# Attention over time and over bands: scores turned to [key, query], exponentials without a maximum, masks as zeros, the division on the output

## The chip, the core and the metric

The kernel runs on one core of one Trainium2 chip. Times are device microseconds of one execution. Three runs of the kernel before took 6690.1, 6692.72 and 6694.46 us; the median, 6692.72, is the time before. Engine names are those of the profile: PE does matmuls (PEld is its loading of weights, a row of its own), ACT the activations, DVE the vector work, POOL is GpSimd, SP issues most of the DMAs.

## What is computed

Input x is [2, 256, 128, 128] float32: batch, time, band, channel. Three residual steps follow each other: causal attention over the 256 time steps of each band, attention over the 128 bands of each time step with a mask of 16 bands to either side, and a feed-forward of width 512.

```python
xt = _ln(x, ln_t_w, ln_t_b).transpose(0, 2, 1, 3)
x = x + _mha(xt, t_wi, t_bi, t_wo, t_bo, 4, causal_mask).transpose(0, 2, 1, 3)
xf = _ln(x, ln_f_w, ln_f_b)
x = x + _mha(xf, f_wi, f_bi, f_wo, f_bo, 4, band_mask)      # |i - j| <= 16
xn = _ln(x, ln_n_w, ln_n_b)
h = gelu(xn @ w1.T + b1)
x = x + (h @ w2.T + b2)
```

In `_mha` queries, keys and values have 4 heads of 32 channels; the weights are softmax(q k^T / sqrt(32) + mask). The weights of the layers are normal with a deviation of 0.02, the biases are 0 and the norms' weights 1. Everything is float32.

## The kernel before, in words

Token tiles are [128 tokens, 128 channels]; four of them (NT = 4) make a unit. In the attention over time a unit is two sequences of 256 steps, in the attention over bands four sequences of 128 bands. Each stage has 128 units. The stages follow each other through an array x1 in HBM.

The function attention (line 134) does a unit. norm_transposed normalises the tiles (statistics and xh on DVE, the power for rstd on POOL), transposes them on PE into the PSUM tile xp, and ACT copies them out as xnT with the norm's weight and bias as scale and bias (131). PE then makes qp, kp and vp (144 to 153); ACT moves qT and kT out with their biases, DVE v. The scores sp are [query, key]: for two heads at a time, PE first writes the mask with a product of a bfloat16 identity and the mask (166) and adds the scores to it (173). DVE takes the negated maximum of each row (181, 187), ACT the exponential with that maximum as bias, 128 or 256 keys at a time, with the row's sum read from its accumulator (195), DVE the reciprocal (203), and POOL multiplies the weights with it (206 over bands, 214 over time). PE transposes every block of 128x128 weights (221), DVE and ACT move the transposed blocks out as pT (226, 228), and PE multiplies with the values (239), which gives op as [channel, query]. ACT moves it out as oT with the values' bias (245), PE makes yp (248), and DVE adds it to rd, or to x2 in the second stage (249).

The first stage loads 8 bands at once and stores a unit's result as it is done. The second works in 32 blocks of 16 time steps (GB): four units of attention, then four of feed-forward (310 to 332), in which PE makes hp, ACT the gelu and PE zp. Because exponential and gelu need different tables in ACT, order_act holds each block's gelus behind its last exponential, and the next block's exponentials behind those.

A scheduler puts the instructions of each engine in order at build time, and each engine then goes through its own list. PSUM has four buffers of one bank for the tiles of the tag ps (xp, qp, kp, vp, tp, op, yp, hp, zp) and two of two banks for sp.

Of the kernel before, what the change touches and what calls it, by code (L numbers as in the profile page):

```python
# [10 lines left out]
BF16 = mybir.dt.bfloat16  # L11
AF = mybir.ActivationFunctionType
# [5 lines left out]
P = 128  # L18
H = 4  # heads
D = 32  # channels of a head  # L20
BAND = 16
EPS = 1e-5
NEG = -1e38  # a masked score, exact enough in bfloat16: its exponential is 0
NT = 4  # token tiles of 128 that are worked on together
GA = 8  # bands loaded at once for the attention over time
GB = 16  # time steps loaded at once for the attention over bands
# [3 lines left out]
def conv_seq_kernel(  # L30
# [13 lines left out]
    """x [B, T, FB, C]; weights transposed to [in, out]; cols [C, 16], the  # L44
    per-channel vectors as columns; rows [3, C], the biases added to token-major
    results."""
    nc = tc.nc
    B, T, FB, C = x.shape
    NI = w1T.shape[1] // P
    NC_T = T // P  # L50
    scale = 1.0 / math.sqrt(D)

    const = ctx.enter_context(tc.tile_pool(name="const", bufs=1))
    xpool = ctx.enter_context(tc.tile_pool(name="xpool", bufs=3))
    work = ctx.enter_context(tc.tile_pool(name="work", bufs=3))
    small = ctx.enter_context(tc.tile_pool(name="small", bufs=6))
    ps_s = ctx.enter_context(tc.tile_pool(name="ps_s", bufs=2, space=PSUM))
    ps = ctx.enter_context(tc.tile_pool(name="ps", bufs=4, space=PSUM))
    dram = ctx.enter_context(tc.tile_pool(name="dram", bufs=1, space=DRAM))

# [1 line left out]
    cols_sb = const.tile([P, 16], F32, name="cols_sb")  # L62
    nc.sync.dma_start(cols_sb, cols)
    rows_sb = const.tile([P, 3, C], F32, name="rows_sb")
    for i in range(3):
        nc.sync.dma_start(rows_sb[:, i, :], rows[i : i + 1, :].partition_broadcast(P).squeeze(1))

    def weight(src, n, name):
        t = const.tile([P, n], F32, name=name)
        nc.scalar.dma_start(t, src)  # L70
        return t

    wiT = (weight(t_wiT, 3 * C, "t_wiT_sb"), weight(f_wiT, 3 * C, "f_wiT_sb"))
    woT = (weight(t_woT, C, "t_woT_sb"), weight(f_woT, C, "f_woT_sb"))
    w1T_sb = weight(w1T, NI * P, "w1T_sb")
    w2T_sb = const.tile([P, NI, C], F32, name="w2T_sb")
    nc.scalar.dma_start(w2T_sb, w2T.rearrange("(j p) c -> p j c", p=P))

    ident = const.tile([P, P], F32, name="ident")
    make_identity(nc, ident)  # L80
    ident_b = const.tile([P, P], BF16, name="ident_b")
    nc.vector.tensor_copy(ident_b, ident)
    mhalf = const.tile([P, NT], F32, name="mhalf")
    nc.vector.memset(mhalf, -0.5)

    # masks for a bank of scores: [query, block, key]
    mask_t = const.tile([P, 3, P], BF16, name="mask_t")
    nc.gpsimd.memset(mask_t, 0.0)
    for n in (0, 2):
        nc.gpsimd.affine_select(  # L90
            out=mask_t[:, n, :], in_=mask_t[:, n, :], compare_op=ALU.is_ge, fill=NEG, base=0,
            pattern=[[-1, P]], channel_multiplier=1,
        )
    mask_f = const.tile([P, NT, P], BF16, name="mask_f")
    nc.gpsimd.memset(mask_f, 0.0)
    for s in (1, -1):
        nc.gpsimd.affine_select(
            out=mask_f, in_=mask_f, compare_op=ALU.is_ge, fill=NEG, base=BAND,
            pattern=[[0, NT], [-s, P]], channel_multiplier=s,
        )  # L100
# [3 lines left out]
    bqs = []  # L104
    for i in (2, 7):
        t = const.tile([P, 1], F32, name=f"bqs{i}")
        nc.vector.tensor_scalar_mul(t, cols_sb[:, i : i + 1], scale)
        bqs.append(t)

    def col(i):  # L110
        return cols_sb[:, i : i + 1]

    def norm_transposed(src, w_col, b_col):
        """Layer norm of four token tiles src(i) [token, C] -> [C, token]."""
        stats = small.tile([P, NT, 6], F32, name="stats")
        mv = small.tile([P, NT, 2], F32, name="mv")
        for i in range(NT):
            nc.vector.bn_stats(stats[:, i, :], src(i))
            nc.vector.bn_aggr(mv[:, i, :], stats[:, i, :])  # L119
        rstd = small.tile([P, NT], F32, name="rstd")  # L120
        nc.gpsimd.tensor_scalar(rstd, mv[:, :, 1], EPS, None, ALU.add)  # L121
        nc.gpsimd.tensor_tensor(rstd, rstd, mhalf, ALU.pow)
        xh = work.tile([P, NT, C], F32, name="xh")
        xp = ps.tile([P, NT * P], F32, name="xp", tag="ps")
        for i in range(NT):
            nc.vector.tensor_scalar(
                xh[:, i, :], src(i), mv[:, i, 0:1], rstd[:, i : i + 1], ALU.subtract, ALU.mult
            )
            nc.tensor.transpose(xp[:, i * P : (i + 1) * P], xh[:, i, :], ident)  # L129
        xnT = work.tile([P, NT * P], F32, name="xnT")  # L130
        nc.scalar.activation(xnT, xp, AF.Identity, bias=col(b_col), scale=col(w_col))  # L131
        return xnT

    def attention(src, dst, which, banks, mask, exp_after):
# [4 lines left out]
        c0 = 5 * which  # L139
        xnT = norm_transposed(src, c0, c0 + 1)  # L140
        wi, wo = wiT[which], woT[which]

        qp = ps.tile([P, NT * P], F32, name="qp", tag="ps")
        nc.tensor.matmul(qp, wi[:, 0:C], xnT, start=True, stop=True)  # L144
        qT = work.tile([P, NT * P], F32, name="qT")
        nc.scalar.activation(qT, qp, AF.Identity, bias=bqs[which], scale=scale)
        kp = ps.tile([P, NT * P], F32, name="kp", tag="ps")
        nc.tensor.matmul(kp, wi[:, C : 2 * C], xnT, start=True, stop=True)  # L148
        kT = work.tile([P, NT * P], F32, name="kT")
        nc.scalar.activation(kT, kp, AF.Identity, bias=col(c0 + 3), scale=1.0)  # L150
        vp = ps.tile([P, NT, C], F32, name="vp", tag="ps")
        for i in range(NT):
            nc.tensor.matmul(  # L153
                vp[:, i], xnT[:, i * P : (i + 1) * P], wi[:, 2 * C : 3 * C], start=True, stop=True
            )
# [214 lines left out]
```

## Time and profile before

| | |
|---|---|
| time, median of three runs | 6692.72 us |
| span of the profiled execution | 6687.7 us |
| mean granted clock of PE | 0.840 |
| HBM read, written | 68.36 MB, 67.11 MB |

The profiled execution's own time is its span and what lies around it; the median is 5.0 us above the span. The page gives each engine's busy time as a share of the span. Since each engine takes its list in order, what matters in a view is what ended the idle time in front of an instruction. In the timeline a row is one run of equal instructions: start in us from the beginning of the span, length, engine, line, operation, output <- inputs, shape, count, and in brackets the idle time before it with the engine and tile that ended it. A float32 product appears on PE as two MATMULs with a LDWEIGHTS each, so a count of 8 stands for four products; a transpose is one. The rows of groups have the same names, then count, busy us in total, mean ns of one, idle time before, and what ended it.

### The profile page before, as it was taken

Reading aid. Unit: us, or ns where it says so; the run is one execution under the profiler, and the core shown is the slowest. Engines: PE = TensorE matmul, PEld = TensorE weight load, DVE = VectorE, ACT = ScalarE, POOL = GpSimd, SP = SyncE. Lnnn points to the kernel's source line nnn. Section 1 sums busy time; section 2 is a strip of 40 time slices with the busy share of each in tenths; the row PEclk is TensorE's granted clock in tenths of the full one; section 3 lists DMA queues with packets and bytes.
Section 4 is the critical chain, followed back from the end, with each engine's and each line's share of the span. In section 5 each row is a group of like instructions: output and inputs, shape, how many; then the busy total and the mean of one; then the engine's idle time right before and its main releaser. Section 6 shows DMA issues by size and latency. Waiting matters only on the chain. (4 is left out here: it accounts for less than half of the span.)

```text
span 6687.7 us, 95401 instructions
## 1 busy us (share of the span) xinstructions
PE 4965.1 (74%) x34688; PEld 3392.3 (51%) x34816; DVE 2769.3 (41%) x8068; ACT 3223.4 (48%) x10688; POOL 2263.4 (34%) x2348
## 2 busy tenths in 40 slices
PE   6777777777777777777777777777676767677767
PEld 4444454444444444454555555555454545455555
DVE  4444444444444444434344444444344444444433
ACT  4444444444444444444454444444444444454544
POOL 4333333333333333433232323233333333233332
PEclk8878787778787877788888888888888888888888
DMA  1000000000000000000000000000000000000000
GB/s 48 20 24 25 23 20 24 24 23 20 24 24 23 20 24 23 24 20 20 24 15 24 14 26 14 26 13 26 13 26 13 26 13 26 13 26 13 20 7 13
DMA packets 222968, 141.61 MB, mean 21 GB/s; under 512 B 7968, under 2 KB 205984, under 8 KB 222496
## 3 DMA queue, kind: packets, MB, share of 16 engines
q1 hardware_dynamic: 221248, 134.45, 7.1%
q8 instruction: 274, 4.49, 0.3%
q14 instruction: 198, 1.62, 0.1%
q10 hardware_dynamic: 1248, 1.05, 0.1%
HBM read 68.36 MB, written 67.11 MB: 20 GB/s over the span
## 5 line engine op out<-in xcount | busy, mean ns | idle before, releaser
L195 ACT ACTIVATE p<-sp,nmax 128x128 f32<-128x128 f32 (+1 forms) x4096 | 1547.6, 414 | 870.0 <-DVE nmax L187 553.6
L221 PE MATMUL tp<-ident,p 128*128 128x128 f32 x5120 | 1207.6, 401 | 275.6 <-POOL p L206 228.0
L221 PEld LDWEIGHTS tp<-ident,p 128*128 128x128 f32 x5120 | 930.1, 209 | 743.0 <-POOL p L206 394.6
L214 POOL TENSOR_TENSOR p<-p,rsum 128x256 f32<-128x256 f32 (+1 forms) x1024 | 823.9, 826 | 952.2 <-DVE rsum L203 820.9
L206 POOL TENSOR_TENSOR p<-p,rsum 128x1024 f32<-128x1024 f32 x256 | 485.2, 1895 | 1493.5 <-DVE rsum L203 1493.5
L195 ACT ACTIVATION_READ_ACCUMULATOR p<-sp,nmax 128x1 f32 x4096 | 929.0, 227 | 0.0
L228 ACT COPY pT<-tp 128x384 f32<-128x384 f32 (+1 forms) x768 | 395.1, 518 | 945.8 <-PE tp L221 942.5
L226 DVE COPY pT<-tp 128x384 f32<-128x384 f32 (+1 forms) x768 | 453.8, 598 | 698.9 <-PE tp L221 689.3
L173 PE MATMUL sp<-kT,qT 32*128 32x128 f32 (+1 forms) x8192 | 740.7, 362 | 0.0
L166 PEld LDWEIGHTS <-ident_b 128*128 128x128 bf16 x1536 | 193.8, 128 | 1007.0 <-issue 663.8
L166 PE MATMUL sp<-mask_t,ident_b 128*128 128x384 bf16 x1024 | 383.1, 472 | 384.6 <-ACT p L195 381.7
L203 DVE RECIPROCAL rsum<-rsum 128x4 f32<-128x4 f32 (+1 forms) x768 | 141.9, 185 | 1221.9 <-ACT p L195 1204.0
L239 PE MATMUL op<-pT,v 128*32 128x128 f32 (+1 forms) x8192 | 526.6, 319 | 86.6 <-DVE pT L226 55.0
L166 PE MATMUL sp<-mask_f,ident_b 128*128 128x512 bf16 x384 | 204.3, 601 | 517.0 <-ACT p L195 517.0
L173 PEld LDWEIGHTS sp<-kT,qT 32*128 32x128 f32 x8192 | 490.8, 214 | 172.9 <-issue 142.1
L317 ACT ACTIVATE hT<-hp,cols_sb 128x512 f32<-128x512 f32 x512 | 351.8, 687 | 392.3 <-PE hp L316 389.5
L187 DVE TENSOR_REDUCE nmax<-sp 128x2 f32<-128x256 f32 (+1 forms) x1024 | 505.0, 545 | 56.6 <-PE sp L173 56.5
L131 ACT ACTIVATE xnT<-xp,cols_sb 128x512 f32<-128x512 f32 x384 | 298.4, 777 | 475.0 <-PE xp L129 475.0
L327 PEld LDWEIGHTS zp<-w2T_sb,hT 128*128 128x128 f32 x4096 | 487.5, 192 | 61.5 <-issue 58.4
L316 PE MATMUL hp<-xnT,w1T_sb 128*128 128x512 f32 x1024 | 471.9, 599 | 42.8 <-ACT xnT L131 27.8
L327 PE MATMUL zp<-w2T_sb,hT 128*128 128x128 f32 x4096 | 499.0, 275 | 0.1
L121 POOL TENSOR_SCALAR rstd<-mv 128x4 f32<-128x4 f32 x384 | 91.8, 242 | 1190.5 <-DVE mv L119 1190.5
(55 smaller groups left out, 5974.5 us busy)
## 6 DMA issues: line engine op xcount, KB each, us to landing
xt<-in_x SPq DMA_DIRECT2D x64, 512.0 KB, 5.5
x<-rd SPq DMA_DIRECT2D x256, 128.0 KB, 1.9
out<-res SPq DMA_DIRECT2D x128, 256.0 KB, 2.3
xb<-x SPq DMA_DIRECT2D x32, 0.5 KB, 6.2
w1T_sb<-in_w1T ACTq DMA_DIRECT2D x1, 256.0 KB, 5.4
w2T_sb<-in_w2T ACTq DMA_DIRECT2D x1, 256.0 KB, 7.1
t_wiT_sb<-in_t_wiT ACTq DMA_DIRECT2D x1, 192.0 KB, 2.5
f_wiT_sb<-in_f_wiT ACTq DMA_DIRECT2D x1, 192.0 KB, 4.5
```

Of the source, the lines that this page charges most:

```text
L166: nc.tensor.matmul(sp[:, j, 0 : nb * P], ident_b, mask.rearrange("p a b -> p (a b)"), start=True, stop=False,)
L173: nc.tensor.matmul(sp[:, j, n * P : (n + len(ks)) * P], qT[r, qi * P : (qi + 1) * P], kT[r, ks[0] * P : (ks[-1] + 1) * P], start=False, st ...
L187: nc.vector.tensor_reduce(nmax[:, :, ri : ri + 1], sp[:, :, n * P : (n + len(ks)) * P], AX.X, ALU.max, negate=True,)
L195: e = nc.scalar.activation(p[:, j, n * P : (n + len(ks)) * P], sp[:, j, n * P : (n + len(ks)) * P], AF.Exp, bias=nmax[:, j, ri : ri + 1], ...
L206: nc.gpsimd.tensor_tensor(pv, pv, rsum.rearrange("p j n -> p (j n)").unsqueeze(2).to_broadcast([P, 2 * nb, P]), ALU.mult,)
L214: nc.gpsimd.tensor_tensor(pv, pv, rsum[:, :, ri : ri + 1].to_broadcast([P, 2, len(ks) * P]), ALU.mult,)
L221: nc.tensor.transpose(tp[:, n * P : (n + 1) * P], p[:, j, n * P : (n + 1) * P], ident)
L226: nc.vector.tensor_copy(t, tp[:, 0 : nb * P])
L228: nc.scalar.copy(t, tp[:, 0 : nb * P])
L239: nc.tensor.matmul(op[r, qi * P : (qi + m) * P], v[:, ki, r], pT[bi, h][:, n * P : (n + m) * P], start=first, stop=last,)
L316: nc.tensor.matmul(hp_, w1T_sb[:, j * P : (j + 1) * P], xnT, start=True, stop=True)
L327: nc.tensor.matmul(zp[:, i], hT[:, j, i * P : (i + 1) * P], w2T_sb[:, j, :], start=(j == 0), stop=(j == NI - 1),)
```

## The change

The program becomes a class with the attention rewritten, and gets a second path.

Setup. The norms' weights are multiplied into the projections, the norms' biases into the projections' biases, 1/sqrt(32) into the queries' weights, and the values' bias through the output projection into rows_sb. For each head a bound on the scores is made on the chip: the sum of the squared norms of the query weights times that of the keys, with the biases' share, compared with LIMIT squared (64 x 64). The eight comparisons are counted; every engine loads the count and branches on it. If all eight hold, the path fast runs; otherwise any_weights, which has the attention of before with loops over bands and over time.

In fast, norm_transposed copies xnT out without scale and bias; qT moves to DVE, v to ACT. Scores are [key, query], all four heads in one PSUM tile sp of four banks, of which there is one buffer. In the time stage of the four blocks of a sequence only that of earlier queries and later keys is left out, as before: 384 columns a head. ACT takes one exponential over a sequence's four heads (128x1536) without a bias, in the band stage two of 128x1024. POOL sets what is masked to 0 in the result, in place, with affine_select. PE multiplies the weights as they are, without a transpose, with the values (op) and with 32 columns of ones (sm), so that each channel's row of sm holds its head's sum. add_attended reads sm with a transposing reduction of DVE, takes 16 reciprocals a partition, spreads and transposes them back to rT, and multiplies op with rT to oT. yp, the addition and the feed-forward are as before.

```diff
-        nc.scalar.activation(xnT, xp, AF.Identity, bias=col(b_col), scale=col(w_col))
+        nc.scalar.copy(xnT, xp)
...
+        nc.vector.tensor_scalar(qT, qp, self.bias[:, 2 * a : 2 * a + 1], None, ALU.add)
...
+        nc.scalar.copy(v, vp)
...
+    def add_attended(self, dst, op, sm, a):
...
+        st = small.tile([P, NT * 4], F32, name="st")
+        nc.vector.tensor_reduce(
+            st, sm.rearrange("p (n k) -> p n k", k=32), AX.X, ALU.max, apply_transpose=True
+        )
+        nc.vector.reciprocal(st, st)
+        rT = work.tile([P, NT * P], F32, name="rT")
+        nc.vector.transpose(
+            rT.rearrange("p (n k) -> p n k", k=32), st.unsqueeze(2).to_broadcast([P, NT * 4, 32])
+        )
+        oT = work.tile([P, NT * P], F32, name="oT")
+        nc.vector.tensor_tensor(oT, op, rT, ALU.mult)
...
+    def weights_time(self, qT, kT, s):
...
+        sp = self.ps_s.tile([P, H, 512], F32, name="sp")
+        for h in range(H):
+            r = slice(h * D, (h + 1) * D)
+            nc.tensor.matmul(
+                sp[:, h, 0 : 2 * P], kT[r, t0 : t0 + P], qT[r, t0 : t0 + 2 * P], start=True, stop=True
+            )
...
+        p = self.pw.tile([P, H, 3 * P], F32, name="p", tag="p")
+        e = nc.scalar.activation(p, sp[:, :, 0 : 3 * P], AF.Exp)
+        for n in (0, 2):
+            d = p[:, :, n * P : (n + 1) * P]
+            nc.gpsimd.affine_select(
+                out=d, in_=d, compare_op=ALU.is_ge, fill=0.0, base=0,
+                pattern=[[0, H], [1, P]], channel_multiplier=-1,
+            )
+        return p, e
+
+    def attention_time(self, src, dst):
+        nc = self.nc
+        qT, kT, v = self.project(src, 0)
+        ps_ = [self.weights_time(qT, kT, s)[0] for s in range(NT // 2)]
...
+            for to, left in ((op, None), (sm, self.ones)):
+                for n, m in ((0, 2), (2, 1)):
+                    for h in range(H):
+                        r = slice(h * D, (h + 1) * D)
+                        nc.tensor.matmul(
+                            to[r, t0 + (2 - m) * P : t0 + 2 * P],
+                            v[:, 2 * s + n // 2, r] if left is None else left,
+                            p[:, h, n * P : (n + m) * P],
+                            start=(n == 0), stop=(n == 2),
+                        )
+        self.add_attended(dst, op, sm, 0)
+
+    def attention_bands(self, src, dst, after):
...
+        for h in range(0, H, 2):
+            e = nc.scalar.activation(p[:, h : h + 2], sp[:, h : h + 2], AF.Exp)
+            self.order_act(e, after)
+            for s in (1, -1):
+                d = p[:, h : h + 2].rearrange("p h (n k) -> p (h n) k", k=P)
+                nc.gpsimd.affine_select(
+                    out=d, in_=d, compare_op=ALU.is_ge, fill=0.0, base=BAND,
+                    pattern=[[0, 2 * NT], [s, P]], channel_multiplier=-s,
+                )
...
+        self.ps_s = ctx.enter_context(tc.tile_pool(name="ps_s", bufs=1, space=PSUM))
+        self.ps = ctx.enter_context(tc.tile_pool(name="ps", bufs=4, space=PSUM))
...
+    with tc.If(bounded > 2 * H - 1) as cmp:
+        with ExitStack() as inner:
+            k.fast(inner)
+    with cmp.Else():
+        with ExitStack() as inner:
+            k.any_weights(inner)
```

The order of instructions is seen best on PE. The second half of a time unit before, from the last mask product to the next unit's transposes (one row is a run of products, the last number is their count):

```order
L166 MATMUL sp<-mask_t,ident_b 128x384
L221 MATMUL tp<-ident,p 128x128 x2
L239 MATMUL op<-pT,v 32x256 x4
L239 MATMUL op<-pT,v 32x128 x4
L239 MATMUL op<-pT,v 32x256 x2
L221 MATMUL tp<-ident,p 128x128 x4
L239 MATMUL op<-pT,v 32x256 x2
L239 MATMUL op<-pT,v 32x128 x4
L248 MATMUL yp<-t_woT_sb,oT 128x128 x4
L129 MATMUL xp<-ident,xh 128x128 x4
```

The same place in the changed program, from the second sequence's scores on (line numbers are those of the changed kernel):

```order
L240 MATMUL sp<-qT,kT 128x256 x4
L245 MATMUL sp<-qT,kT 128x128 x4
L270 MATMUL op<-p,v 32x256 x4
L270 MATMUL op<-p,v 32x128 x4
L270 MATMUL sm<-p,ones 32x256 x4
L270 MATMUL sm<-p,ones 32x128 x4
L270 MATMUL op<-p,v 32x256 x4
L270 MATMUL sm<-p,ones 32x256 x4
L270 MATMUL op<-p,v 32x128 x4
L270 MATMUL sm<-p,ones 32x128 x4
L205 MATMUL yp<-t_woT_sb,oT 128x128 x4
L161 MATMUL xp<-ident,xh 128x128 x4
```

Transposes and mask products are gone, each op product has a sm product beside it, and as before nothing of the next unit stands ahead of yp.

A band unit on PE in the changed program, from its scores to the next unit's transposes:

```order
L286 MATMUL sp<-qT,kT 128x128 x16
L304 MATMUL op<-pb,v 32x128 x2
L306 MATMUL sm<-pb,ones 32x512 x2
L304 MATMUL op<-pb,v 32x128 x14
L306 MATMUL sm<-pb,ones 32x512 x2
L205 MATMUL yp<-f_woT_sb,oT 128x128 x4
L161 MATMUL xp<-ident,xh 128x128 x4
```

Only two op and two sm products, those of heads 0 and 1, stand ahead of the first op of heads 2 and 3.

DVE between two band units, before, from the addition of one unit's yp to the next unit's evacuation:

```order
L249 TENSOR_TENSOR x_37106<-yp,x_37106 128x512
L118 BN_STATS stats<-x_37106 128x6 x4
L119 BN_AGGR mv<-stats 128x2 x4
L126 TENSOR_SCALAR xh<-x_37106,mv,rstd 128x128 x4
L157 COPY v<-vp 128x512
L181 TENSOR_REDUCE nmax<-sp 128x8 x2
L203 RECIPROCAL rsum<-rsum 128x8 x2
L226 COPY pT<-tp 128x512 x2
```

And in the changed program, third and fourth unit of a block:

```order
L206 TENSOR_TENSOR x_17830<-yp,x_17830 128x512
L150 BN_STATS stats<-x_17830 128x6 x4
L151 BN_AGGR mv<-stats 128x2 x4
L158 TENSOR_SCALAR xh<-x_17830,mv,rstd 128x128 x4
L174 TENSOR_SCALAR qT<-qp,bias 128x512
L193 TENSOR_REDUCE st<-sm 128x16
L196 RECIPROCAL st<-st 128x16
L198 STREAM_TRANSPOSE rT<-st 128x512
L202 TENSOR_TENSOR oT<-op,rT 128x512
```

The place where v was moved out, behind the feed-forward's xh, is now that of qT; in the second unit of a block qT stands ahead of xh.

More of the change, by code (lines that the diff above doesn't have):

```diff
@@ L11 @@
 BF16 = mybir.dt.bfloat16
+I32 = mybir.dt.int32
 AF = mybir.ActivationFunctionType
@@ L43, in conv_seq_kernel @@
 ):
[L47 to L84, printed above, removed]
@@ L87, in conv_seq_kernel @@
[L87 to L100, printed above, removed]
@@ L104, in conv_seq_kernel @@
[L104 to L132, printed above, removed]
@@ L336 @@
+    k = Kernel(tc, ctx, x, t_wiT, t_woT, f_wiT, f_woT, w1T, w2T, cols, rows, out)
+    bounded = tc.nc.values_load(
+        k.count[0:1, 0:1], min_val=0, max_val=2 * H,
+        skip_runtime_bounds_check_because="a count of 2 H comparisons",
+    )
+    with tc.If(bounded > 2 * H - 1) as cmp:
[4 more added lines that the diff above has]
+            k.any_weights(inner)
 def kernel(**inputs):
```

571 lines of the change are left out of this document (390 added, 181 removed).

## The prediction

> **What bounds the kernel now.** First the page: busy shares, then the granted clock in 40 slices (tenths of full speed).
>
> ```profile
> span 6687.7 us, 95401 instructions
> PE 4965.1 (74%) x34688; PEld 3392.3 (51%) x34816; DVE 2769.3 (41%) x8068; ACT 3223.4 (48%) x10688; POOL 2263.4 (34%) x2348
> PEclk8878787778787877788888888888888888888888
> ```
>
> PE is the busiest engine, at three quarters, and its clock is cut in every slice. Next, one unit of the attention over time in PE's timeline (start, us, line, operation, count, idle before it and who ended it). One unit is four token tiles; there are 128 in each of the two stages.
>
> ```profile
> 1503.62 0.60 PE L129 MATMUL xp<-ident,xh 128*128 128x128 f32 x4
> 1505.09 1.12 PE L144 MATMUL qp<-xnT,t_wiT_sb 128*128 128x512 f32 x2 [0.87 <-ACT xnT L131]
> ...
> 1507.89 0.95 PE L173 MATMUL sp<-kT,qT 32*128 32x128 f32 x16
> 1511.77 0.48 PE L166 MATMUL sp<-mask_t,ident_b 128*128 128x384 bf16 x2 [2.93 <-ACT p L195]
> ...
> 1515.84 2.40 PE L221 MATMUL tp<-ident,p 128*128 128x128 f32 x10
> ...
> 1524.93 1.16 PE L248 MATMUL yp<-t_woT_sb,oT 128*128 128x128 f32 x8 [0.78 <-ACT oT L245]
> ```
>
> The unit is a chain: PE works through one unit before the next and idles where ACT or DVE answers. Its length over the stage comes from the tile rd (count, duration, first and last start):
>
> ```profile
> L249 DVE TENSOR_TENSOR rd<-yp,rd x128: 690/691/692, 44.2 to 3075.5; 128x512 f32<-128x512 f32 x128
> ```
>
> (3075.5 − 44.2) / 127 = 23.87 us a unit, 3055 for 128. The rest, 6687.7 − 3076 = 3611, is 32 blocks of 112.8: four units of attention over bands and four of feed-forward. A band unit, and the end of one block's feed-forward:
>
> ```profile
> 4023.19 1.72 PE L173 MATMUL sp<-kT,qT 32*128 32x128 f32 x32
> 4028.67 0.54 PE L166 MATMUL sp<-mask_f,ident_b 128*128 128x512 bf16 x1 [3.76 <-ACT p L195]
> ...
> 4036.43 1.06 PE L239 MATMUL op<-pT,v 128*32 128x128 f32 x26 [0.38 <-ACT pT L228]
> 4038.27 1.16 PE L248 MATMUL yp<-f_woT_sb,oT 128*128 128x128 f32 x8 [0.78 <-ACT oT L245]
> ```
>
> ```profile
> 4059.62 0.60 PE L129 MATMUL xp<-ident,xh 128*128 128x128 f32 x4
> 4091.61 0.59 PE L144 MATMUL qp<-xnT,f_wiT_sb 128*128 128x512 f32 x1
> ```
>
> Four feed-forward units take 4091.61 − 4059.62 = 32.0 us. The clock, by stretches (length, then busy PE, PEld, DVE, ACT, POOL, then granted clock):
>
> ```profile
> 1508.00:1513.00 5.00, 2.07 (x26) 1.15 (x26) 2.82 (x6) 3.00 (x15) 1.48 (x3) 1.00 0.01 2
> 1513.00:1520.00 7.00, 7.00 (x33) 5.24 (x32) 3.65 (x10) 4.61 (x20) 4.18 (x6) 0.51 0.00 0
> ...
> 4025.00:4028.50 3.50, 0.00 (x0) 0.10 (x1) 1.75 (x2) 2.79 (x17) 0.00 (x0) 1.00 0.01 2
> 4028.70:4035.60 6.90, 5.16 (x19) 3.49 (x19) 1.73 (x4) 3.29 (x17) 3.79 (x2) 0.51 0.01 2
> 4062.00:4090.00 28.00, 27.62 (x161) 20.04 (x160) 15.39 (x56) 14.44 (x21) 12.31 (x12) 1.00 0.10 29
> ```
>
> A stretch in which PE works under half the time is followed by some 7 us at half clock; a full one (feed-forward) keeps full clock. So an idle PE costs twice.
>
> **The change, part by part.** Per time unit PE loses 8 mask products and 24 transposes with their evacuations, ACT loses 16 small exponentials with 16 accumulator reads, DVE the maxima, POOL the product with the reciprocals. The new order is still one unit after the other, so the new unit is again a chain. Its prices:
>
> ```profile
> L195 ACT ACTIVATE p<-sp,nmax 128x256 f32<-128x256 f32 x1024 | 490.3, 479 | 0.0
> L317 ACT ACTIVATE hT<-hp,cols_sb 128x512 f32<-128x512 f32 x512 | 351.8, 687 | 392.3 <-PE hp L316 389.5
> L228 ACT COPY pT<-tp 128x512 f32<-128x512 f32 x256 | 149.8, 585 | 468.2 <-PE tp L221 468.2
> L131 ACT ACTIVATE xnT<-xp,cols_sb 128x512 f32<-128x512 f32 x384 | 298.4, 777 | 475.0 <-PE xp L129 475.0
> L97 POOL TENSOR_SCALAR_AFFINE_SELECT mask_f<-mask_f 128x512 bf16<-128x512 bf16 x2 | 1.3, 634 | 0.1
> L90 POOL TENSOR_SCALAR_AFFINE_SELECT mask_t<-mask_t 128x128 bf16<-128x128 bf16 x2 | 0.5, 292 | 0.0
> masks.py:199 POOL TENSOR_SCALAR_AFFINE_SELECT ident<-ident 128x128 f32<-128x128 f32 x1 | 0.3, 292 | 0.0
> L206 POOL TENSOR_TENSOR p<-p,rsum 128x1024 f32<-128x1024 f32 x256 | 485.2, 1895 | 1493.5 <-DVE rsum L203 1493.5
> L301 POOL TENSOR_TENSOR x<-xb,rows_sb 128x2048 f32<-128x2048 f32 x32 | 145.6, 4550 | 4.8 <-DMA xb<-x 2.4
> L187 DVE TENSOR_REDUCE nmax<-sp 128x2 f32<-128x512 f32 x512 | 348.0, 680 | 0.0
> L203 DVE RECIPROCAL rsum<-rsum 128x4 f32<-128x4 f32 x512 | 90.0, 176 | 608.0 <-ACT p L195 590.2 <-POOL p L214 17.9
> L203 DVE RECIPROCAL rsum<-rsum 128x8 f32<-128x8 f32 x256 | 51.9, 203 | 613.9 <-ACT p L195 613.9
> ```
>
> ACT takes 208 ns per 256 elements more, so an exponential of 1536 costs 687 + 832 = 1.5 us, one of 1024 1.1. Masking in place on float32 is not in the trace; at 128 elements both types cost 292 ns and the slope is 0.89 ns an element, so 512 cost 0.63 and 1024 1.09 us. Bounds: 0.8 of that below, the product of L206 (1.9) above; I stay with the same operation. DVE's transposing reduction and the 32x32 transposes are not in the trace either: I take 0.68 and 0.69 like plain passes over 512 (from half to double), the reciprocal of 16 as 0.26.
>
> *Time unit at full clock, from the start of xp:* to qp 1.47 − (0.78 − 0.59) = 1.28, since the copy takes no scale and bias; qp, kp, vp 2.80 (1507.89 − 1505.09; kT ends beside vp, and qT, now on DVE, before it); scores of the first sequence 0.95 (same eight products); its exponential 1.5 and 0.1 of handover, which nothing on PE hides, because the one score buffer must be read before the second sequence's scores; these 0.95; second exponential 1.6, under which PE does the first sequence's op and sm; one of its two masks 0.7, the other beside PE; op and sm 1.7 (26 instructions with 3328 columns took 1.06, here 6144 columns, less what is pipeline end); then reduction, reciprocal, transpose and product on DVE 0.68 + 0.26 + 0.69 + 0.69 + 0.1 = 2.4, where 0.78 stood; yp 1.00. Sum 15.0.
>
> *Half clock:* PE idles 5.7 of these 15 us, the tail of 2.4 next to 0.7 for xnT. I charge each unit one stretch like the present one, 6.8 us, of which 0.7 is waiting: half of 6.1, 3.0. Unit 18.0, stage 2304: **−751**.
>
> *Band unit at full clock:* 1.28 + 2.80; scores 1.1, four heads in turn instead of two (from 0.95 to 1.72); exponential 1.2; then POOL's four masks in one queue, 4.4, since the second exponential ends under the first two masks and the last op waits for the last mask; op and sm behind them 2.0; tail 2.4; yp 1.0: 16.2. In units three and four DVE has xh ahead of qT, and xh waits for POOL's power:
>
> ```profile
> 4019.11 0.69 DVE L249 TENSOR_TENSOR x<-yp,x 128x512 f32<-128x512 f32 x1 [3.76 <-PE yp L248]
> ...
> 4022.50 1.11 DVE L126 TENSOR_SCALAR xh<-x,mv,rstd 128x128 f32<-128x128 f32 x4 [1.51 <-POOL rstd L122]
> ```
>
> xh ends 4.7 us after xp began (4018.91, at 4038.27 + 1.00 one unit earlier), qT 0.7 later, scores 1.3 later than at 4.1: 17.5. The first unit has xnT ready but waits 0.2 for the exponentials' table: 15.1. Block: 15.1 + 16.2 + 2 × 17.5 + 31.8 = 98.1. A gap of 5.6 with 1 us of work always trips the clock; what follows at half clock is op, sm, yp, xp and part of qp to vp, 7.2 us of doubled work, +3.6 a unit. Block 112.5 against 112.8: **−11**. Here the gain is eaten by POOL's queue and the clock.
>
> ```profile
> L122 POOL TENSOR_TENSOR rstd<-rstd,mhalf 128x4 f32<-128x4 f32 x384 | 399.7, 1047 | 26.1
> L282 POOL TENSOR_TENSOR rd<-xt,rows_sb 128x512 f32<-128x512 f32 x128 | 162.2, 1268 | 45.1 <-DMA x<-rd 36.5 <-DMA xt<-in_x 8.5
> ```
>
> *What I cost at nothing:* qT on DVE and v on ACT in the time stage, and the reads of statistics: ACT has 0.59 + 0.69 + 0.59 + 3.0 = 4.9 us of work in a unit of 15, DVE 2.3 in the tail and 0.69 + 0.69 + 1.1 for qT, yp's addition and xh, and statistics; what they do there lies beside qp to vp or beside the scores. If that cover went, as it does in band units three and four, each unit would pay up to 1.3. POOL's power and addition for later units (1.0 and 1.3) run before the first masks are due at 6.5 us after xp. The loads and stores keep their places on SP's queue behind the same waits. *What the new waits hold up:* behind the first op that waits for a mask PE has the rest of op and sm, yp and the next unit's xp in its queue, so every wait for POOL in a band unit goes straight into the unit. Behind the wait of yp for DVE's product stands the next xp, although its input has long been there: nothing fills the tail. Four PSUM banks turn round for seven tiles a unit; op and sm are held through the tail, and the next to want op's bank is the next unit's qp, by then free.
>
> *Setup:* the chain of small products on PE and DVE, the flag's load and the branch now precede the loads of x. Statistics began at 10.1:
>
> ```profile
> 10.11 1.26 DVE L118 BATCH_NORM_STATS2 stats<-xt 128x6 f32<-128x128 f32 x6 [6.82 <-DMA xt<-in_x]
> ```
>
> 36 DVE instructions at 0.2 to 0.5, partly beside the weights' loads, and a load of 7 behind them: **+25** (15 to 50). Sum: 6687.7 − 751 − 11 + 25 = 5951 for the profiled execution's span; the median lies 5.0 above the span: 5956.
>
> **A rule weighed.** The half clock at 1513 to 1520 followed a gap of only 2.93 us. The Trainium skill, "TensorE: Matmul & The Clock Gate", § HAM oscillation, asks only for no idle gaps over about 3.4 us. By that the time units, with gaps up to 2.4, would stay at full clock; the trace disagrees for now, but the half-busy threshold is not sharp in it, so this is the first rival. For the masks, "GPSIMD Engine Reference", § 4.1 Engine selection, puts one-input operations of GpSimd at roughly line rate and two-input ones at about twice VectorE's time; 634 ns for a mask of 512 beside DVE's 680 for a reduction of 512 agrees, which speaks for the low price.
>
> **Rivals.** *Full clock in the time stage*: 15.0 a unit, 384 less: 5570. For it: no gap reaches 2.93. Against: 62% busy on average, less around the tail. *Half clock almost throughout*: another 2.5 a unit, 20.5: 6275. For it: the tail, xnT and the first exponential each leave PE idle. *POOL's masks become the bound, slower than before*: a mask of 1024 that costs x more adds 4x in a band unit and about x in a time unit (two masks of half the size on its path), 640x in all. At L206's price, x = 0.8: 6470. At L301's 2.22 ns an element, 2.3 a mask, x = 1.2: 6720, slower; it decides at x = 1.15. Against: three rows of the same operation. *The second path runs*: the flag compares the product of squared weight norms with 4096; weights of deviation 0.02 give per head 32 × 128 × 0.0004 × 136 = 223 for keys, a 32nd of it for queries, product 1550, so the first path runs. The second has the old attention in loops with fewer buffers: over 6900.
>
> **Chances.** Forecast 0.55; full clock 0.17; half clock 0.18; masks 0.07, of which 0.05 slower than before; second path 0.03. Range: from full clock in the time stage to half clock throughout with masks or DVE's transposes dearer by 0.25: 5550 to 6450. About 0.2% is what can be told from no change: faster 0.91, same 0.01, slower 0.08.
>
> **What would show it.** A time unit of 18 us between two yp with PE idle 2.4 before yp; granted clock about 0.75 there and no better in the band units; exponentials of 1.5 and masks of 0.63 and 1.09; PE waiting for POOL's mask before the last op; a block still near 112. Wrong would be: masks near 2 us, the tail over 3.5, or products of four heads that do not overlap.

## The result, and the profile after

The changed kernel takes 5929.14 us, median of four runs (5916.78 to 5935.99), beside 6693.59 us (6690.1 to 6695.26) for the kernel before on the same chip: a ratio of 0.8856, 95% interval 0.8844 to 0.8869. The profiled execution has a span of 5915.1 us; the prediction for it was 5951. First the page: span, busy shares, and the granted clock in 40 slices.

```profile
span 5915.1 us, 79997 instructions
PE 4105.8 (69%) x33318; PEld 2701.9 (46%) x33318; DVE 2042.5 (35%) x6314; ACT 1603.7 (27%) x1984; POOL 1805.4 (31%) x2086
PEclk9888888888888788778777887877787787788778
```

ACT's work has halved, PE's has fallen by a sixth, and yet every engine is busy for a smaller share than before: the kernel still waits. The clock has become better in the first 15 slices (the time stage) and worse behind them; in the kernel before, it was 0.79 in the time stage and 0.88 in the second (last number but two of these rows, laid out as in the prediction):

```profile
100.00:3000.00 2900.00, 2241.84 (x14559) 1433.47 (x14559) 1225.07 (x3613) 1375.62 (x4869) 1093.63 (x1336) 0.79 0.08 23
3200.00:6500.00 3300.00, 2378.43 (x17689) 1719.40 (x17807) 1353.34 (x3860) 1622.89 (x5100) 1022.89 (x851) 0.88 0.07 19
```

The tile rd (durations, first and last start) gives the time stage:

```profile
L206 DVE TENSOR_TENSOR rd<-yp,rd x128: 691/692/693, 47.8 to 2235.4; 128x512 f32<-128x512 f32 x128
```

(2235.4 − 47.8) / 127 = 17.23 us a unit, 6.64 less than before. The span's 772.6 us less split into +3.6 up to the first rd, −843.7 over these 127 intervals, and +67.5 from the last rd to the end (3612.2 before, 3679.7 now): 115.0 us a block of the second stage, 2.1 more than before. PE's timeline over one time unit (start, length, idle before it and who ended it):

```profile
1018.15 1.64 PE L205 MATMUL yp<-t_woT_sb,oT 128*128 128x128 f32 x8 [2.60 <-DVE oT L202]
1019.58 1.06 PE L161 MATMUL xp<-ident,xh 128*128 128x128 f32 x4
1021.32 2.07 PE L172 MATMUL qp<-xnT,t_wiT_sb 128*128 128x512 f32 x2 [0.67 <-ACT xnT L163]
...
1028.75 1.14 PE L240 MATMUL sp<-qT,kT 32*128 32x256 f32 x8 [1.65 <-ACT p L249]
...
1036.76 1.16 PE L205 MATMUL yp<-t_woT_sb,oT 128*128 128x128 f32 x8 [2.60 <-DVE oT L202]
1037.76 0.60 PE L161 MATMUL xp<-ident,xh 128*128 128x128 f32 x4
```

The unit is a chain of PE and the engines that answer it, with the waits of the forecast: 0.67 for xnT, 1.65 for the exponential, 2.60 for DVE's tail. The same xp takes 1.06 us at 1019.58 and 0.60 at 1037.76. The busy time in stretches around it (length, PE, PEld, DVE, ACT, POOL, granted clock) shows why:

```profile
1015.25:1018.66 3.41, 0.81 (x16) 0.54 (x9) 2.37 (x4) 0.00 (x0) 0.00 (x0) 1.00 0.00 0
1018.66:1025.48 6.82, 6.15 (x17) 3.67 (x17) 2.94 (x10) 0.93 (x2) 2.49 (x3) 0.50 0.14 38
1025.48:1028.90 3.42, 1.77 (x27) 1.44 (x29) 0.00 (x0) 2.37 (x3) 0.13 (x1) 1.00 0.00 0
1028.90:1032.31 3.41, 3.41 (x40) 2.18 (x44) 0.00 (x0) 1.45 (x1) 1.43 (x3) 0.50 0.00 0
1032.31:1035.72 3.41, 1.85 (x44) 1.02 (x36) 1.42 (x3) 0.00 (x0) 0.88 (x2) 1.00 0.02 5
1035.72:1039.14 3.42, 1.70 (x13) 1.47 (x13) 2.08 (x6) 0.58 (x1) 0.00 (x0) 1.00 0.00 0
1039.14:1042.55 3.41, 3.41 (x28) 2.31 (x28) 1.72 (x8) 1.27 (x2) 1.54 (x3) 1.00 0.27 77
...
100.00:2200.00 2100.00, 1407.35 (x14627) 935.57 (x14625) 734.12 (x2151) 579.82 (x609) 606.80 (x849) 0.83 0.12 32
2400.00:5800.00 3400.00, 2433.06 (x16571) 1589.14 (x16572) 1170.96 (x3684) 920.59 (x1246) 1080.11 (x1093) 0.79 0.06 18
```

The stretch that holds the tail has PE busy for 0.81 of 3.41 us, and the next 6.82 us run at half clock; one with 1.77 of 3.42, which holds the exponential's wait, is followed by 3.41 at half clock. One with 1.70 of 3.42 is not: half busy is about the edge, and not a sharp one. Over the stages the clock is 0.83 (time) and 0.79 (bands). The groups with the new operations (busy, mean ns, idle time before and who ended it):

```profile
L294 POOL TENSOR_SCALAR_AFFINE_SELECT pb<-pb 128x1024 f32<-128x1024 f32 x512 | 541.0, 1091 | 1154.0 <-ACT pb L290 1154.0
L304 PE MATMUL op<-pb,v 128*32 128x128 f32 x4096 | 372.6, 409 | 611.7 <-POOL pb L294 611.7
L249 ACT ACTIVATE p<-sp 128x1536 f32<-128x1536 f32 x256 | 371.2, 1450 | 210.8 <-PE sp L245 200.2 <-POOL p L252 9.5 <-POOL rd L333 1.2
L252 POOL TENSOR_SCALAR_AFFINE_SELECT p<-p 128x512 f32<-128x512 f32 x512 | 313.2, 634 | 487.3 <-ACT p L249 487.2
L205 PE MATMUL yp<-t_woT_sb,oT 128*128 128x128 f32 x1024 | 205.8, 363 | 341.4 <-DVE oT L202 341.4
L216 PE MATMUL hp<-xnT,w1T_sb 128*128 128x512 f32 x1024 | 521.0, 651 | 39.0 <-ACT xnT L163 23.4 <-DVE res L228 15.6
```

PE waits 611.7 / 128 = 4.8 us in each band unit for POOL's masks, and 341.4 / 128 = 2.7 in each time unit for DVE's tail. A band unit, over all engines:

```profile
3066.87 1.17 PE L286 MATMUL sp<-qT,kT 32*128 32x128 f32 x32
3068.17 1.94 ACT L290 ACTIVATE pb<-sp 128x1024 f32<-128x1024 f32 x2 [0.61 <-PE sp L286]
3069.26 4.23 POOL L294 TENSOR_SCALAR_AFFINE_SELECT pb<-pb 128x1024 f32<-128x1024 f32 x4 [5.86 <-ACT pb L290]
3072.50 0.64 PE L304 MATMUL op<-pb,v 128*32 128x128 f32 x4 [4.46 <-POOL pb L294]
3077.28 0.72 DVE L193 TRANSPOSE_TENSOR_REDUCE st<-sm 128x16 f32<-128x512 f32 x1 [11.79 <-PE sm L306]
3079.81 1.65 PE L205 MATMUL yp<-f_woT_sb,oT 128*128 128x128 f32 x8 [2.58 <-DVE oT L202]
```

Four masks in one queue, 4.23 us; the first op starts as the third ends (3069.26 + 3 × 1.06), since POOL does the two halves in turn. Op and sm then take 4.8 us at half clock.

### The profile page after: what moved, and what is told of

It is laid out like the page before. It is cut to its first block, busy times and chain, and to the rows that moved or that the text cites. A ratio compares the mean times of both kernels' runs of the same rounds, so it can differ in the third digit from the quotient of the medians.

```text
span 5915.1 us, 79997 instructions
## 1 busy us (share of the span) xinstructions
PE 4105.8 (69%) x33318; PEld 2701.9 (46%) x33318; DVE 2042.5 (35%) x6314; ACT 1603.7 (27%) x1984; POOL 1805.4 (31%) x2086
## 3 DMA queue, kind: packets, MB, share of 16 engines
q10 hardware_dynamic: 1248, 1.05, 0.1%
## 5 line engine op out<-in xcount | busy, mean ns | idle before, releaser
L294 POOL TENSOR_SCALAR_AFFINE_SELECT pb<-pb 128x1024 f32<-128x1024 f32 x512 | 541.0, 1091 | 1154.0 <-ACT pb L290 1154.0
L304 PE MATMUL op<-pb,v 128*32 128x128 f32 x4096 | 372.6, 409 | 611.7 <-POOL pb L294 611.7
L217 ACT ACTIVATE hT<-hp,bias 128x512 f32<-128x512 f32 x512 | 351.9, 687 | 458.9 <-PE hp L216 458.4
L205 PE MATMUL yp<-f_woT_sb,oT 128*128 128x128 f32 x1024 | 234.2, 402 | 330.4 <-DVE oT L202 330.4
L252 POOL TENSOR_SCALAR_AFFINE_SELECT p<-p 128x512 f32<-128x512 f32 x512 | 313.2, 634 | 487.3 <-ACT p L249 487.2
L205 PE MATMUL yp<-t_woT_sb,oT 128*128 128x128 f32 x1024 | 205.8, 363 | 341.4 <-DVE oT L202 341.4
L306 PE MATMUL sm<-pb,ones 128*32 128x512 f32 x1024 | 442.4, 962 | 0.0
L249 ACT ACTIVATE p<-sp 128x1536 f32<-128x1536 f32 x256 | 371.2, 1450 | 210.8 <-PE sp L245 200.2
L154 POOL TENSOR_TENSOR rstd<-rstd,mhalf 128x4 f32<-128x4 f32 x384 | 403.5, 1053 | 16.2
L158 DVE TENSOR_SCALAR xh<-xb,mv,rstd 128x128 f32<-128x128 f32 x512 | 273.0, 596 | 326.0 <-PE xp L161 234.9
L270 PE MATMUL op<-p,v 128*32 128x256 f32 (+1 forms) x4096 | 281.9, 376 | 89.1 <-POOL p L252 89.1
```

Source lines behind the costliest of these rows:

```text
L154: nc.gpsimd.tensor_tensor(rstd, rstd, self.mhalf, ALU.pow)
L158: nc.vector.tensor_scalar(xh[:, i, :], src(i), mv[:, i, 0:1], rstd[:, i : i + 1], ALU.subtract, ALU.mult)
L205: nc.tensor.matmul(yp[:, i], oT[:, i * P : (i + 1) * P], self.wo[a], start=True, stop=True)
L217: e = nc.scalar.activation(hT[:, j, :], hp, AF.Gelu, bias=self.bias[:, 4 + j : 5 + j], scale=1.0)
L249: e = nc.scalar.activation(p, sp[:, :, 0 : 3 * P], AF.Exp)
L252: nc.gpsimd.affine_select(out=d, in_=d, compare_op=ALU.is_ge, fill=0.0, base=0, pattern=[[0, H], [1, P]], channel_multiplier=-1,)
```

## The experiments

Three theories went into them. **A:** a unit's length is PE's chain of waits, and each half-idle stretch costs a second time through the clock. **B:** PE's amount of work sets the time, and the gain came from the products and transposes left out. **C:** the granted clock does not depend on these gaps. Two sets of runs of the changed kernel itself gave medians of 5929 and 5903 us, so differences below some 30 us between sets are not told apart.

**Filling the time unit.** Products that nobody needs, whose PSUM tile the real products then overwrite: one behind the first sequence's scores, two behind the last sum. The next xp stays behind yp as before.

```diff
+        for _ in range(GAP):                 # 1, into op, behind the first scores
+            f = nc.tensor.matmul(op, self.ident, qT, start=True, stop=True)
...
+            for _ in range(FILL[a]):         # 2, into yp, behind the last sm
+                f = nc.tensor.matmul(yp.rearrange("p n c -> p (n c)"), self.ident, qT, start=True, stop=True)
```

> Time stage only: three products of 128x512 that nobody needs are put into PE's idle stretches, one behind the first sequence's scores (idle 1.66 us) and two behind the last sum (idle 2.60 us), 2.6 us more PE work per unit at full clock. Theory A (a unit is PE's chain of waits, lengthened by half clock after half-idle stretches): the idle time is not lengthened, the clock stays full, the unit falls from 17.2 to about 15.1 us, 128 x 2.1 = 270 less: 5660 us, granted clock near 1.00 in the time stage. Theory B (PE's amount of work sets the time): 128 x 2.6 = 330 more: 6260 us. Theory C (the granted clock does not depend on these gaps): units stay at 17.2, clock 0.84: 5930 us, or up to 100 more where a product overruns its gap at half clock.

Measured 5695.46 us (ratio to the kernel before 0.8502, 0.8488 to 0.8517): 234 less than the changed kernel, with 384 float32 products more. Its tile rd, the time stage by stretches, and two rows of a fourth unit:

```profile
L228 DVE TENSOR_TENSOR rd<-yp,rd x128: 691/692/693, 48.1 to 2024.4; 128x512 f32<-128x512 f32 x128
```

```profile
100.00:2000.00 1900.00, 1504.88 (x15373) 912.37 (x15372) 726.27 (x2156) 580.96 (x611) 607.97 (x847) 0.99 0.13 35
```

```profile
985.53 3.33 DVE L161 BATCH_NORM_STATS2 stats<-xt 128x6 f32<-128x128 f32 x16 [6.29 <-DMA xt<-in_x]
...
991.29 1.16 PE L226 MATMUL yp<-t_woT_sb,oT 128*128 128x128 f32 x8 [1.86 <-DVE oT L215]
```

Clock 0.99 instead of 0.83, and three units in four now take 15.06 us, the forecast's chain at full clock (15.0). B and C fall: more work, less time, and the clock follows the gaps. The mean is (2024.4 − 48.1) / 127 = 15.56, because every fourth unit mostly has 16 to 17: there the statistics of a load that has just landed, 16 in a row for 3.33 us, stand in DVE's queue ahead of the tail, and yp waits 1.86 instead of the usual 0.68.

**Only the tail filled** (the same with GAP left out).

> As in the run that filled both idle stretches of the time unit, but only the tail is filled (two products of 128x512 behind the last sum), the wait for the first exponential (1.66 us) stays idle. Theory A: the tail, where PE does 1.0 us of work in 3.4, is what trips the clock; the stretch around the exponential is about half busy (two times 0.95 in 3.5 us) and lies at the edge: 15.1 to 15.6 us a unit, 5690 to 5760 us. If the exponential's wait alone is enough to trip it: units as now, 5930 us or more.

Measured 5701.42 us (0.852, 0.8506 to 0.8535), as with both:

```profile
L227 DVE TENSOR_TENSOR rd<-yp,rd x128: 691/692/693, 46.9 to 2023.1; 128x512 f32<-128x512 f32 x128
```

```profile
100.00:2000.00 1900.00, 1416.28 (x15148) 900.76 (x15144) 726.27 (x2156) 580.43 (x611) 608.54 (x849) 0.96 0.13 35
```

15.56 us a unit, at a clock of 0.96. So in the time stage it is the tail's half clock that costs the time. The exponential's 1.65 us trips the clock too: by the trace's clock records, 45 of the 141 falls to half clock in the changed kernel's time stage (100 to 2200 us) follow a window of 3.41 us whose longest wait is for the exponential, the other 96 one for the tail. With the tail filled 32 falls behind the exponential are left (100 to 2000 us), and they do not make the unit longer than with both filled.

**Filling the band units** in the same way, three products behind the scores and two behind the last sum.

```diff
+        for _ in range(GAPB):                # 3, into op, behind the scores of a band unit
+            f = nc.tensor.matmul(op, self.ident, qT, start=True, stop=True)
```

> Band units only: three products of 128x512 that nobody needs behind the scores (PE idle 4.46 us for POOL's masks) and two behind the last sum (idle 2.58 us), 4.3 us more PE work per unit at full clock. Theory A: after the first unit of a block the clock stays full; the unit falls from 20.5 to about 16 us (1.28 + 2.80 + 1.1 + exponential 1.2 + masks 4.2 + rest of op and sm 1.5 + tail 2.5 + yp 1.0 = 15.6), feed-forward enters at full clock, a block falls from 115.0 to 96 to 98 us: 32 x 18 = 580 less: 5350 us. Theory B: 128 x 4.3 = 550 more: 6480 us. Theory C: 5930 us.

Measured 5344.96 us (0.7982, 0.7969 to 0.7996), 584 less. The band stage by stretches, and one unit:

```profile
2400.00:5300.00 2900.00, 2503.14 (x17991) 1535.73 (x17980) 1193.74 (x3720) 932.65 (x1260) 1093.34 (x1109) 0.99 0.08 22
```

```profile
3052.76 1.17 PE L308 MATMUL sp<-qT,kT 32*128 32x128 f32 x32
3053.86 2.84 PE L311 MATMUL op<-qT,ident 128*128 128x512 f32 x6
3058.39 0.41 PE L330 MATMUL op<-pb,v 128*32 128x128 f32 x4 [1.69 <-POOL pb L321]
3063.94 1.16 PE L226 MATMUL yp<-f_woT_sb,oT 128*128 128x128 f32 x8 [0.67 <-DVE oT L215]
3064.93 0.60 PE L172 MATMUL xp<-ident,xh 128*128 128x128 f32 x4
```

Clock 0.99 instead of 0.79. Blocks, from one first hp to the next, take 95.9 to 97.9 us instead of 115.0 on average, and band units two to four 16.3 instead of 20.6 (units three and four of the changed kernel), although POOL's masks and DVE's tail are as long as before. (5341.5 − 2244.1) / 32 = 96.8 a block: the clock cost 18 us a block.

**The order of the masks.** POOL does both masks of heads 0 and 1 first, and PE op and sm in the same order.

```diff
+                if h > 0 and s > 0:
+                    self.pin(k, before)     # keeps POOL's order; before is the mask emitted last
+                before = k
...
+        for h0 in range(0, H, 2):           # op and sm of heads h0, h0 + 1, then the others
```

> POOL applies both masks of heads 0 and 1 before those of heads 2 and 3 (in the changed kernel the two halves alternate, so that the first op waits for the third mask), and PE does op and sm of heads 0 and 1 ahead of heads 2 and 3. Theory A: op starts one mask (1.05 us) earlier and the first half of op and sm (about 2 us at half clock) lies under the last two masks: 1.0 to 1.6 us less per band unit, 4 to 6.5 per block, 130 to 210 less: 5720 to 5800 us; if block lengths go in steps of a clock window of 3.41 us, 1 or 2 steps. Theory D (the last mask alone sets the unit, as the prediction had it, and what stands ahead of it is hidden anyway): within 30 us of 5930.

Measured 5830.31 us (0.8706, 0.8677 to 0.8736), 99 less; the second stage is 3578.4 us instead of 3679.7, 3.2 a block. One op of it:

```profile
3070.22 1.07 PE L315 MATMUL op<-pb,v 128*32 128x128 f32 x16 [3.53 <-POOL pb L301]
```

PE waits 3.53 us instead of 4.46. The order is on the path, so D falls, but the gain, 0.8 a unit, is half to three quarters of A's; the clock stays low, 0.829 over the run beside 0.811. POOL's order and PE's were changed together, so their parts are not told apart.

**Division left out.** DVE multiplies op with the copied sums.

```diff
-        nc.vector.tensor_reduce(
-            st, sm.rearrange("p (n k) -> p n k", k=32), AX.X, ALU.max, apply_transpose=True
-        )
-        nc.vector.reciprocal(st, st)
...
+        nc.vector.tensor_copy(rT, sm)
```

> The division is left out: instead of reduction, reciprocal and transpose (716 + 253 + 711 ns) DVE copies the sums (about 0.6 us) and multiplies by them; all products on PE stay. Theory A: the tail between the last sum and yp is 1.0 to 1.1 us shorter in all 256 units, and PE's idle stretch with it: at least 256 x 1.05 = 270 less, 5660 us; with fewer half-clock windows down to 5450. Theory B (PE's amount of work sets the time): 5930 us.

Measured 5082.52 us (0.7589, 0.7576 to 0.7602): 847 less, where A had counted 270 for the tail and at most some 200 more for the clock. Two stretches and the tail of a unit:

```profile
100.00:1800.00 1700.00, 1125.02 (x14030) 757.67 (x14024) 587.75 (x1868) 555.78 (x585) 580.91 (x818) 0.96 0.14 37
2200.00:5000.00 2800.00, 1972.38 (x15817) 1315.84 (x15815) 1002.22 (x3265) 878.48 (x1186) 1028.18 (x1043) 0.88 0.08 21
```

```profile
1019.49 1.16 PE L198 MATMUL yp<-t_woT_sb,oT 128*128 128x128 f32 x8 [1.55 <-DVE oT L195]
```

The tail's gap is 1.55 instead of 2.60 us, the products on PE are the same, and the clock rises to 0.96 and 0.88. Units take 14.0 us in the time stage (15.06 − 1.05) and 16.6 to 17.7 in the bands. One us of waiting taken away was worth 847 / (256 × 1.05) = 3.2.

**qT on ACT again in the band units.**

```diff
+        if a:
+            nc.scalar.activation(qT, qp, AF.Identity, bias=self.bias[:, 2 * a : 2 * a + 1], scale=1.0)
```

> In the band units qT's bias addition is on ACT again instead of DVE, where in units three and four it stands behind xh. The prediction's step (scores 1.3 us later in two units of four): 32 x 2 x 1.3 = 83 less: 5845 us. The reading of the trace (at half clock the products of q, k and v end after qT anyway): within 20 us of 5930, a little more if kT on ACT now comes behind qT.

Measured 5920.95 us (0.8848, 0.8832 to 0.8863): no change that can be told. The prediction's +1.3 in units three and four was not there to be won.

**Setup.** Four kernels: without the branch and the second path, twice; the changed kernel again; and the branch without a second path.

```diff
-    with tc.If(bounded > 2 * H - 1) as cmp:
-        with ExitStack() as inner:
-            k.fast(inner)
-    with cmp.Else():
-        with ExitStack() as inner:
-            k.any_weights(inner)
+    with ExitStack() as inner:
+        k.fast(inner)
```

> The flag is computed but not read: the fast path stands without branch and without the second path. Theory A: the loads of x start some 13 us earlier, the first xp about 10 us earlier, everything behind unchanged: 5919 us. The prediction's price of the setup (25): 5904 us. Theory E (the branch costs code loading or queue work along the whole program too): under 5890 us.

Measured 5903.82 us (0.8814, 0.8799 to 0.8829), 25 below the changed kernel's first set, while the profiled span was only 3.4 shorter (the profiled execution was the slowest of its four here, and the fastest of the changed kernel's). To settle that, side by side, five runs each:

> The changed kernel itself, for a direct comparison with the next two: 5915 to 5935 us.

> The flag computed and not read, no branch and no second path, once more beside the changed kernel. Theory A (the setup costs what the start of the first time unit shows, 2.5 to 3.4 us): within 10 us of the changed kernel. Theory E (25 us, partly outside the profiled span): 20 to 30 us less.

> The flag is read and the branch taken, but there is no second path, so the program is shorter by it. If theory E holds and it is the second path's code that costs, this is 20 to 30 us under the changed kernel; if the branch costs, it equals the changed kernel; under theory A all three lie within 10 us.

Measured 5902.58, 5905.73 and 5915.14 us (ratios 0.8819, 0.8819 and 0.8826, each interval 0.0012 to 0.0015 to either side). The changed kernel came out 12 us under its expectation, and the three do not differ. The branch and the second path cost nothing that can be told; the 25 us were the spread between sets.

**Useful work instead of filling.** The same operations, but work of unit n+1 stands between the parts of unit n, in both stages; add_attended is split into the division and the output for that, and p and rd get four buffers instead of three. On PE the order is not quite the one expected below. In the time stage the projections of unit n+1 stand ahead of op and sm of unit n, and its scores behind these, around yp of unit n. In the bands the scores of unit n+1 stand behind most of op of unit n, ahead of its sums and its yp.

```diff
+            qT, kT, v = self.project(None, 0, xnT)
+            if prev is not None:
+                oT = self.attended_time(*prev[1:])      # op, sm, division of the unit before
+            p0 = self.weights_time(qT, kT, 0)[0]
+            ...
+                xnT = self.norm_transposed(nxt[0])
+            p1 = self.weights_time(qT, kT, 1)[0]
+            if prev is not None:
+                self.add_output(prev[0][1], oT, 0)      # yp and the addition
```

> The same operations in another order: projections and scores of unit n+1 are issued before op, sm and the output of unit n, in both stages, so that useful products stand in PE's queue where it waited for exponentials, masks and DVE. Theory A: a time unit is 2.8 + 1.9 + 0.95 + 0.6 + 0.9 (rest of the tail) + 1.0 + 0.95 = 9.1 us at full clock, 8.1 less, 1040 in all; a band unit is bound by PE or POOL (masks 4.2 + rstd 1.3 + res 1.3 = 6.8), about 8, so a block is 4 x 8 + 6 for filling and draining + 32 = 70 instead of 115, 1440 less: 3450 us, up to 3800 if exponentials or masks stay on the path. Theory B: 5930 us, or not under the 4106 us that PE is busy now.

Measured 4149.35 us (0.6196, 0.6186 to 0.6207), 1780 less than the changed kernel: A's direction, but 350 above the upper end of its sum. A row of its page, its tile rd, and two rows of the timeline:

```profile
PE 3376.3 (81%) x33318; PEld 2313.3 (56%) x33318; DVE 2108.3 (51%) x6314; ACT 1577.0 (38%) x1984; POOL 1801.3 (43%) x2086
```

```profile
L214 DVE TENSOR_TENSOR rd<-yp,rd x128: 655/678/692, 53.3 to 1707.6; 128x512 f32<-128x512 f32 x128
```

```profile
627.56 1.65 DVE L150 BATCH_NORM_STATS2 stats<-xt 128x6 f32<-128x128 f32 x8 [6.61 <-DMA xt<-in_x]
...
634.79 2.05 PE L213 MATMUL yp<-t_woT_sb,oT 128*128 128x128 f32 x8 [7.88 <-DVE oT L206]
```

The same 33318 matmuls keep PE busy for 3376 us instead of 4106, so B's floor was itself made of half clock; the next kernel goes below it. A time unit takes (1707.6 − 53.3) / 127 = 13.0 us, not 9.1: most about 11 to 12, every fourth mostly 16 to 19, where the statistics of a new load block DVE as above, now for 7.88 us of PE. In a quick one (11.04 us from yp at 709.73 to yp at 720.77) PE still waits 1.24 for DVE's product and 0.45 for a mask, which the sum of 9.1 left out. A block takes (4153.4 − 1707.6) / 32 = 76.4, not 70.

**Statistics kept back.** In the time stage DVE takes a unit's statistics only behind the division two units before it.

```diff
+            if i == 0 and after is not None:
+                self.order_act(m, after)     # m: first bn_stats; after: the product oT two units back
```

> The pipelined order, and in the time stage DVE takes the statistics of a unit only after the division two units before it. In the pipelined run every fourth time unit took 16 to 19 us, because statistics of a load just issued stood in DVE's queue ahead of the tail (7.88 us of idle PE before yp). Theory A (PE's wait is DVE's queue behind the load): these units fall to 11 to 13 us, 31 x 5 = 155 less, a bit more from the clock: 3950 to 4000 us. Rival (the loads themselves come too late, on SP's queue behind the stores): within 30 us of 4149.

Measured 3981.88 us (0.5947, 0.5938 to 0.5956), 167 less, as A had it: DVE's queue was what held PE, not the loads. (1553.5 − 49.4) / 127 = 11.8 us a unit by

```profile
L216 DVE TENSOR_TENSOR rd<-yp,rd x128: 660/691/693, 49.4 to 1553.5; 128x512 f32<-128x512 f32 x128
```

with most units at 10.7. From yp to yp, 74 of 127 take under 10.9 us and 31 take 13 or more. In these 31 PE waits 2.9 us on average for POOL's masks, in the 74 hardly at all; why the masks come late there was not looked into.

## Why the prediction was right, point by point

**The mechanism held.** It forecast a chain per unit, made longer by half clock, and not a time set by PE's work. The two fillings show both halves of it: work added into the gaps made the kernel faster, and the chain came out as worked out, within 0.1 us in the time unit. Two signs that the prediction named did not come: the clock in the time stage was 0.83, not about 0.75, and a block went to 115.0 instead of staying near 112.

**The time unit's chain at full clock** was 15.0; 15.06 was measured. The prices in it held: exponentials 1450 ns for 1.5, masks 634 for 0.63, the tail's gap 2.60 for 2.4 and handover.

**Half clock in the time unit** was the term sized too large: 3.0 a unit, for one stretch like that of before in each. By the chain at full clock it was 17.23 − 15.06 = 2.2, of which the filling took away 17.23 − 15.56 = 1.67. The stretches at half clock are 3.41 or 6.82 us long, and some units have full clock throughout (15.06 occurs in the changed kernel too). The 0.5 between 15.56 and 15.06 goes with something the prediction had at nothing, the statistics ahead of the tail: in the filled kernel yp waits over 0.3 us longer than usual in 29 of 128 units. In the changed kernel it does so in only 8. Together −844 instead of −751. No run fills the gaps of the kernel before, so how much of this is the shorter chain and how much the better clock (0.79 to 0.83) is not told apart.

**The band block** was wrong in sign: +2.1 a block where −0.35 stood (112.5 against 112.8). The chain at full clock was rather shorter than forecast: 16.3 in each of units two to four for 16.2, 17.5 and 17.5, and a block at 95.9 to 97.9 for 98.1. The step of qT behind xh (+1.3 twice a block) was not there: with full clock in the filled kernel units three and four are no longer than unit two, and moving qT to ACT changed nothing. The first unit, on the other hand, was priced too low: the prediction had 0.2 for the exponentials' table, but its load waits for the scores and then takes 1.28 us on the path, as here in the changed kernel:

```profile
3044.81 1.28 ACT L290 ACT_TABLE_LOAD   x1 [0.59 <-PE sp L286]
```

The masks' step held in its sum and not in its parts: op starts behind the third mask, not the last, and takes correspondingly longer. What failed is the price of the clock, 3.6 a unit or 14.4 a block: it was 20.6 − 16.3 = 4.3 a unit, and feed-forward, which the prediction left at 31.8, begins at half clock too (hp's mean rose from 599 to 651 ns; with the gaps filled it is 596). Together 115.0 − 96.8 = 18.2 a block, so +67 instead of −11.

**The setup** was priced at 25 (15 to 50). Statistics begin 10.5 us later (20.6 instead of 10.1). The first rd starts only 3.6 us later than before, since from the first statistics to it takes 27.2 us instead of 34.1: the first unit is shorter too. Neither the branch nor the second path's code can be told in the time.

**The sum** came out 36 us above the span because the three errors nearly cancel, and that is luck: −93 in the time stage, +78 in the bands, −21 in the setup (with the first unit's own saving, some 7 us, counted here).

**The rivals.** Full clock in the time stage: the clock was 0.83, so no, though PE's waits for the tail are under 2.7 us in all but 11 of 128 units. Of these the longest is 3.93. The Trainium skill, "TensorE: Matmul & The Clock Gate", § HAM oscillation, which asks only for no idle gap over about 3.4 us, does not agree with this trace: the half clock at 1018.66 followed a stretch with a gap of 2.60. Half clock throughout: no. Dear masks: 634 and 1091 ns, as interpolated. The second path was not taken.

## What to carry to other kernels

Where a window of 3.4 us leaves PE idle for half of it or more, and a gap of 2.6 us is enough for that, a us of waiting can cost more than itself. In two runs here it was worth 3.2 us (the division) and some 0.9 (the masks' order). Price the wait and the half clock that follows it, and test it by filling the gap with products nobody needs, which is two lines of code. Then replace the filling with the next unit's work, and look at what each in-order queue has ahead of the instruction on the path: a mask of the other half or an early statistic is enough to stop PE.

## What the runs showed of the hardware

In these traces the granted clock is either full or half and changes in steps of 3.413 us, the unit of the trace's clock records (3.41 and 6.82 in the stretches above). How busy PE was in the window before decides, and the gap need not fill the window. Counted over the changed kernel's whole trace, half clock followed 338 of the 350 windows at full clock in which PE was busy for under 0.44 of the time, 46 of 134 between 0.44 and 0.53, and none of 584 above. At half clock, full clock followed all 323 windows with PE busy for over 0.9 and none of 74 under 0.7.

A block's length tends to whole numbers of such steps. From one block's first hp to the next, 29 of the 31 blocks of the kernel before lie within 112.4 to 113.2 us, which is 33 steps (112.6). In the changed kernel 11 of 31 do, and the other 20 lie within 115.8 to 116.4, which is 34 steps (116.05). So the second stage's +2.1 a block is about two blocks in three with one step more. With the masks' order 15 of 31 lie at 33 steps, none at 34, and the others off the steps, from 108.4 to 114.6. That small changes in the bands come out as nothing or as a whole step fits the run with qT on ACT, but it was not tested.
